# A graph attention kernel: node inputs and target logits in one DRAM row, one broadcast load for the turned rows, loads in another order

## The chip, the core and the metric

The kernel runs on one core of a Trainium2 chip. The metric is the device time of one execution in microseconds (us). PE is TensorE, DVE VectorE, ACT ScalarE, POOL GpSimd and SP SyncE, which here only issues DMAs. Before the change three runs took 2981.59, 2987.33 and 2987.8 us, a median of 2987.33.

## The reference, cut to what matters

There are 12,500 nodes with 128 inputs each and 200,000 edges, sorted by their destination `dst`; N and E are these two numbers.

```python
h = maximum(layernorm(x), 0)
hn = (h @ W_node.T).reshape(N, 4, 32)              # 4 heads of 32
e = (edge_attr @ W_edge.T).reshape(E, 4, 32)
att = sum(concat([hn[src], hn[dst], e], -1) * a, -1)
att = where(att > 0, att, 0.2 * att)
m = maximum(segment_max(att, dst), 0)
ex = exp(att - m[dst])
denom = segment_sum(ex, dst) + (E - deg)[:, None] * exp(-m)
w = ex / denom[dst]
out = x + segment_sum(w[:, :, None] * hn[src], dst).reshape(N, 128)
```

Here `deg` is the number of edges that end in a node.

## The kernel before, in words

A logit is a sum of a source part, a target part and an edge part, so the first two are made once for each node. The node stage (`load_nodes`, `node_statistics`, `node_scaled`, `turn_nodes`, `node_values`) goes through 11 sets of up to 9 tiles of 128 nodes: it loads x (L356), normalizes it, multiplies by the weights on PE, and stores two tables to DRAM. `table` has 137 floats a node: the values of the four heads, ones, and the source logits. `tgt` has the target logit as three bf16 pieces of four heads, 24 bytes a node (L394 to L399).

Edges are cut into 392 groups of 511, each with a leading slot that carries the group before over, 512 slots in all. Four groups make a quad (98 quads). Four quads make a round with one softmax (fewer at both ends; 28 rounds). The destinations of a group lie in a window of 96 nodes, whose first node is a number in SBUF (`base`); SP reads it into a register (L465) to address its loads and stores.

POOL gathers the rows of the source nodes: 16 indirect DMAs a quad (L135) into one of 8 buffers. The first four quads are gathered from x instead, before the node tables exist, and converted on the core (`converted`). A buffer comes free when its quad's last sum has been made (L638).

`fetch(q)` issues the loads of a quad on SP, two quads ahead of the logits: the edges' inputs `ea` (L472, 512 KB), the destinations broadcast to 96 partitions `db` (L474, 768 KB), and for each of the four groups the window's target logits `sw` (L480, 96 rows of 24 bytes) and the window's rows of x, `xw` (L481, 96 rows of 512 bytes). `db` has two buffers: its load waits until the comparison of the quad two back has read it (DVE L505). `xw` has eight.

`logits(q, i)` makes one group's logits: DVE compares destinations with the window (L505, into `at`), PE multiplies `at` by `sw` (L510) and the edges by their weights (L513). `add_sources` adds the gathered source part. `softmax(s)` handles a round: logits are turned on PE so that edges lie along the free axis, running maxima are scanned on DVE with the help of `dr`, the destinations in rows, which `fetch_rows` loads with four DMAs of the same rows, one a head (L489); exponentials are made on ACT and turned back (L601, L609).

`sums(q)` then takes a quad's four groups: DVE scales the gathered rows (L661) and makes the one-hot matrix (L664), and PE sums rows by destination (L669, three of four matmuls). The fourth (L638, in `complete_group`) needs the previous group's last row, which ACT takes out of PSUM (L639) and DVE scales (L633). `divide` makes the quad's output, adds x from `xw` (L692), and stores it with four DMAs (L694), each of which waits for the one before, since windows overlap.

The order of the work is written out by hand: generators are stepped in turn by `together`, and each engine runs its instructions in the order in which they were recorded. In the steady part one step pairs `sums(p)` with `all_logits(p + 5)`, whose first act is `fetch(p + 7)`; the closing quad of a round has `softmax` in the same step. On SP a step is therefore the loads of `fetch(p + 7)`, then the four stores of quad p - 1.

Of the kernel before, what the change touches and what calls it, by code (L numbers as in the profile page):

```python
# [8 lines left out]
F32 = mybir.dt.float32  # L9
BF16 = mybir.dt.bfloat16  # L10
# [5 lines left out]
P = 128  # L16
# [15 lines left out]
QG = 4  # L32
SBG = 16
PIECES = 3
NODE_T = 9
RAW = 4
SETS = max(NODE_T, QG * J)
# [8 lines left out]
def kernel(  # L46
# [42 lines left out]
    dram = ctx.enter_context(tc.tile_pool(name="dram", bufs=1, space=bass.MemoryType.DRAM))  # L89

    table = dram.tile([NP, ROW], F32, name="table")
    tgt = dram.tile([NP, PIECES, H], BF16, name="tgt")

    ident = consts.tile([P, P], F32, name="ident")
    make_identity(nc, ident)
# [50 lines left out]
    with tc.manual_schedule():  # L146
# [32 lines left out]
        def statistics(pool, rows, T):  # L179

            stats = pool.tile([P, SETS, nc.vector.BN_STATS_DIM], F32, name="stats")
            mv = pool.tile([P, SETS, nc.vector.BN_AGGR_DIM], F32, name="mv")
            for t in range(T):
                nc.vector.bn_stats(stats[:, t, :], rows[:, t, :])
                nc.vector.bn_aggr(mv[:, t, :], stats[:, t, :])  # L185
                if t % 3 == 2 or t == T - 1:
                    yield
            rstd = pool.tile([P, SETS], F32, name="rstd")
            nc.scalar.activation(rstd[:, :T], mv[:, :T, 1], AF.Sqrt, bias=eps)
            nc.vector.reciprocal(rstd[:, :T], rstd[:, :T])  # L190
# [69 lines left out]
        with tc.tile_pool(name="node", bufs=2) as node, tc.tile_pool(  # L260
# [91 lines left out]
            def load_nodes(b):  # L352
                if b < len(sets):
                    t0, T = sets[b]
                    XT[b] = node.tile([P, NODE_T, D], F32, name="xt", bufs=4)
                    nc.sync.dma_start(XT[b][:, :T, :], by_tile(x, t0, T))  # L356

            def node_statistics(b):
                if b < len(sets):
                    MV[b] = yield from statistics(node, XT[b], sets[b][1])  # L360

            def node_scaled(b):
                if b < len(sets):
                    HN[b] = node.tile([P, NODE_T, D], F32, name="hn", bufs=2)
                    yield from scaled(HN[b], XT.pop(b), sets[b][1], *MV.pop(b))

            waiting = []

# [9 lines left out]
            def node_values():  # L378
                b, t1, m, hT, row = waiting.pop(0)
                row_ps = node_ps.tile([P, 512], F32, name="row_ps")  # L380
                row_ps = row_ps[:, 0:3 * 160].rearrange("p (t r) -> p t r", r=160)
                for t in range(m):
                    nc.tensor.matmul(row_ps[:, t, :TCOL], hT[:, t, :], wcat, start=True, stop=True)  # L383
                nc.scalar.copy(row[:, t1:t1 + m, :], row_ps[:, :m, :TCOL])
                t0, T = sets[b]
                if t1 + m < T:
                    return
                one = row[:, :T, 0:H * HW].rearrange("p t (h w) -> p t h w", w=HW)[:, :, :, HD]
                nc.vector.memset(one, 1.0)
                nc.vector.memset(row[:, :T, R_CNT:R_CNT + 1], 1.0)  # L390
                nc.sync.dma_start(by_tile(table, t0, T), row[:, :T, 0:ROW])
                tp = node.tile([P, NODE_T, PIECES, H], BF16, name="tp")
                tg = row[:, :T, ROW:TCOL]
                for k in range(PIECES):  # L394
                    nc.vector.tensor_copy(tp[:, :T, k, :], tg)
                    if k < PIECES - 1:
                        nc.vector.tensor_tensor(tg, tg, tp[:, :T, k, :], op=OP.subtract)
                nc.scalar.dma_start(by_tile(tgt.rearrange("n k h -> n (k h)"), t0, T),
                                    tp[:, :T].rearrange("p t k h -> p t (k h)"))  # L399

            for b in range(3):
                load_nodes(b)
# [42 lines left out]
    with tc.tile_pool(name="load", bufs=3) as load, tc.tile_pool(name="work", bufs=2) as work, \  # L445
            tc.tile_pool(name="turned", bufs=1) as turned, \
            tc.tile_pool(name="ps", bufs=1, space=bass.MemoryType.PSUM) as ps:
        EA, DB, SW, XW, LG, AT, U, DR = {}, {}, {}, {}, {}, {}, {}, {}


        const_ps = ps.tile([P, WIN + G + QG * H], F32, name="const_ps")
# [17 lines left out]
        def fetch(q):  # L469
            g0, m = quads[q]  # L470
            ea = EA[q] = load.tile([P, QG, 2, P], F32, name="ea")
            nc.sync.dma_start(ea[:, :m], edge_t[:, g0:g0 + m])  # L472
            db = DB[q] = load.tile([WIN, QG, GE], I32, name="db", bufs=2)
            nc.sync.dma_start(db[:, :m, :], dst.rearrange("(g e) -> g e", e=GE)[g0:g0 + m]  # L474
                              .unsqueeze(0).to_broadcast([WIN, m, GE]))
            sw = SW[q] = load.tile([WIN, QG, PIECES * H], BF16, name="sw")
            xw = XW[q] = load.tile([WIN, QG, D], F32, name="xw", bufs=8)
            for i in range(m):
                w = window(g0 + i)
                nc.sync.dma_start(sw[:, i, :], tgt[bass.ds(w, WIN)].rearrange("n k h -> n (k h)"))  # L480
                nc.sync.dma_start(xw[:, i, :], x[bass.ds(w, WIN), :])  # L481
            if q not in GA:
                gather(q, table, ROW)

        def fetch_rows(s):
            g0, m = groups(s)
            dr = DR[s] = turned.tile([SBG * H, NE + 2], I32, name="dr", bufs=2)
            for h in range(H):
                nc.sync.dma_start(dr[h * m:(h + 1) * m, :], dst_rows[g0:g0 + m, :])  # L489

        def open_logits(q):
            if q == supers[of_quad[q]][0]:
# [6 lines left out]
        def logits(q, i):  # L499

            g0, m = quads[q]
            if i >= m:
                return
            ea, db, sw, at, lg = EA[q], DB[q], SW[q], AT[q], LG[q]
            nc.vector.tensor_tensor(  # L505
                at[:, i, :], node_ps[0:WIN, g0 + i:g0 + i + 1].to_broadcast([WIN, GE]), db[:, i, :],
                op=OP.is_equal)
            for w in range(2):
                for j in (2 * w, 2 * w + 1):
                    nc.tensor.matmul(lg[:, i, j].rearrange("p k h -> p (k h)"),  # L510
                                     at[:, i, j * P:(j + 1) * P], sw[:, i, :],
                                     start=i + j == 0, stop=False, skip_group_check=True)
                nc.tensor.matmul(lg[:, i, 2 * w:2 * w + 2, 0, :], ea[:, i, w, :], wblk,  # L513
                                 start=False, stop=True, skip_group_check=True)

        def add_sources(q):

            s = of_quad[q]
            g0, m = quads[q]
            s0, sm = groups(s)  # L520
            if s not in U:
                U[s] = turned.tile([P, J, SBG * H], F32, name="U", bufs=2)
            u = U[s][:, :, 0:sm * H].rearrange("p j (h g) -> p g j h", h=H)[:, g0 - s0:g0 - s0 + m]
            st = work.tile([P, QG, J, H], F32, name="st")
            nc.vector.tensor_reduce(st[:, :m], LG[q][:, :m].rearrange("p g j k h -> p g j h k"),
                                    AX.X, OP.add)
            nc.vector.tensor_tensor(u, st[:, :m], GA[q][:, :m, :, R_SRC:R_SRC + H], op=OP.add)
            for kept in (EA, DB, SW, AT, LG):
                del kept[q]

        XS = {}
# [142 lines left out]
        def divide(q, pt):  # L674
# [14 lines left out]
            nc.vector.tensor_tensor(  # L689
                res[:, :m, :].rearrange("p g (h d) -> p g h d", d=HD), val[:, :, :, 0:HD],  # L690
                share_ps[:, :m, :].unsqueeze(3).to_broadcast([WIN, m, H, HD]), op=OP.mult)
            nc.vector.tensor_tensor(res[:, :m, :], res[:, :m, :], xw[:, :m, :], op=OP.add)  # L692
            for i in range(m):
                nc.sync.dma_start(out[bass.ds(window(g0 + i), WIN), :], res[:, i, :])  # L694

# [50 lines left out]

    redo = nc.values_load(flag[0:1, 0:1], min_val=0, max_val=1)
    with tc.If(redo > 0):
        tile_any_order(tc, x, src, dst, edge_t, table, tgt, wblk, ident, part, out, by_tile, E)


@with_exitstack
def tile_any_order(ctx, tc, x, src, dst, edge_t, table, tgt, wblk, ident, part, out, by_tile, E):

# [31 lines left out]
    with tc.For_i(0, EP // (2 * P), 1) as pair:  # L786
# [4 lines left out]
        for c in range(2):  # L791
# [5 lines left out]
            nc.vector.tensor_scalar(dfl, di, float(NP - 1), None, op0=OP.min)  # L797
            nc.vector.tensor_copy(di, dfl)
            ga = pool.tile([P, ROW], F32, name="any_ga")
            tg = pool.tile([P, PIECES * H], BF16, name="any_tg")  # L800
            st = pool.tile([P, ROW], F32, name="any_st")
            for o, i, ix in ((ga, table, si), (tg, tgt.rearrange("n k h -> n (k h)"), di),
                             (st, states[0:NP], di)):
                nc.gpsimd.indirect_dma_start(
                    out=o, out_offset=None, in_=i,
                    in_offset=bass.IndirectOffsetOnAxis(ap=ix[:, 0:1], axis=0))
# [4 lines left out]
            att = pool.tile([P, H], F32, name="any_att")  # L811
            nc.vector.tensor_tensor(att, lg[:, c, :], ga[:, R_SRC:R_SRC + H], op=OP.add)
            for k in range(PIECES):
                nc.vector.tensor_tensor(att, att, tg[:, k * H:(k + 1) * H], op=OP.add)
            nc.vector.scalar_tensor_tensor(att, att, SLOPE, att, op0=OP.mult, op1=OP.max)


# [125 lines left out]
```

## Time and profile before

| what | us |
|---|---|
| median of three runs | 2987.33 |
| the profiled execution | 3018.5 |
| its span | 3016.7 |
| first gathers, from x (64) | 2.9 to 82.8 |
| first gathers from `table` (64) | 185.3 to 265.5 |
| the other 1438 gathers, in batches of 16 | 339.9 to 2873.0 |

In a line of groups or of the timeline, `out<-in` are the program's tile names, and brackets hold the engine's idle time before the instruction and what ended it. In a line of waits the numbers are the total in us, the times and the longest. A line of the busy times by stretch has the stretch, its length, then busy us and number of instructions of PE, PE's weight loads, DVE, ACT and POOL, the granted clock of PE, the busy share of the 16 DMA engines, and GB/s. "remote" stands for a wait whose end the trace can't put down to an instruction or a DMA. Rows named SPq are DMA issues on SP; a register move or a register load is not shown in the timeline, but is in the trace. A batch's distance is from one batch's first gather to the next one's.

### The profile page before, as it was taken

The page shows a single profiled execution, that of the slowest core. Times are in us where ns is not written, and L with a number is a line of the kernel's source. Part 1 is how long each engine was busy: PE and PEld are TensorE (multiplying, and loading weights), DVE is VectorE, ACT ScalarE, POOL GpSimd, SP SyncE. Part 2 cuts the span into 40 slices and gives each one's busy share as a digit, 9 for nine tenths or more (in the row PEclk, how much of TensorE's full clock was granted, in tenths as well). Part 3 has the DMA queues.
Part 4 walks back from the last instruction along what each step waited for, and adds up shares of the span by engine and source line. Part 5 has one row for each costly group of instructions (what it writes and reads, how often), then busy time and mean ns, then how long its engine had stood idle before and what let it go on. Part 6 is the DMA issues. An engine that isn't in the chain of part 4 may idle for free.

```text
span 3016.7 us, 29229 instructions
## 1 busy us (share of the span) xinstructions
PE 1411.3 (47%) x7275; PEld 1268.1 (42%) x7275; DVE 1381.7 (46%) x3438; ACT 424.0 (14%) x1764; POOL 1498.2 (50%) x1574
## 2 busy tenths in 40 slices
PE   1541645444444544544544444454454444444464
PEld 1431544344444444434434444444444444444354
DVE  1741454444544544544444443454454444444466
ACT  1431311111110111111111111011111111111111
POOL 7043245556556555555555555555555555555500
PEclk9755655555555555555555555555555555555555
DMA  3632454344344344444444434434444344444320
GB/s 113 115 75 70 110 126 107 94 108 110 96 102 109 97 100 110 101 104 102 102 103 103 107 98 104 108 96 105 106 105 106 97 110 103 98 108 101 83 57 15
DMA packets 228078, 299.11 MB, mean 99 GB/s; under 512 B 89081, under 2 KB 177273, under 8 KB 218498
## 3 DMA queue, kind: packets, MB, share of 16 engines
q1 hardware_dynamic: 174512, 184.67, 23.9%
q0 software_dynamic: 50112, 109.65, 16.2%
q10 hardware_dynamic: 3282, 2.89, 0.4%
q8 instruction: 61, 1.00, 0.1%
q14 instruction: 111, 0.91, 0.1%
HBM read 270.49 MB, written 26.52 MB: 98 GB/s over the span
## 4 chain that ended last, share of the span: by engine, by line
another core or an unknown queue 30%; PE 29%; DVE 12%; issue 9%; ACT 5%; ACTq 0%; DMA 0%; SPq 0%; DVEq 0%
PE acc L669 15%; PE lg L513 6%; PE acc L638 5%; DVE res L689 2%; DVE at L505 2%; DVE res L692 2%; ACT pt L639 2%; DVE run L578 1%; PE lg L510 1%; PE t_ps L547 1%; ACT ga L657 1%; DVE run L556 1%; ACT ga L637 1%; DVE top L584 1%
## 5 line engine op out<-in xcount | busy, mean ns | idle before, releaser
L135 POOL DMA_INDIRECT ga<-table,srci x1502 | 1436.6, 956 | 1353.6 <-PE acc L638 817.6
L669 PE MATMUL acc<-ga,hot 128*97 128x137 f32 x2352 | 652.8, 450 | 753.5 <-ACT ga L657 648.6
L669 PEld LDWEIGHTS acc<-ga,hot 128*97 128x97 f32 x2352 | 523.3, 281 | 778.3 <-ACT ga L657 656.8
L633 DVE TENSOR_TENSOR ga<-pt,facs 1x132 f32<-1x132 f32 x391 | 112.3, 287 | 988.5 <-ACT pt L639 797.0
L639 ACT COPY pt<-acc 97x137 f32<-97x137 f32 x392 | 107.5, 274 | 2144.4 <-remote 1087.1
L513 PE MATMUL lg<-wblk,ea 128*128 128x8 f32 x1568 | 408.7, 359 | 0.0
L510 PEld LDWEIGHTS <-at 96*128 96x128 bf16 x1568 | 214.8, 166 | 423.2 <-DVE at L505 246.8
L513 PEld LDWEIGHTS lg<-wblk,ea 128*128 128x128 f32 x1568 | 381.7, 309 | 0.0
L510 PE MATMUL lg<-sw,at 96*128 96x12 bf16 x1568 | 169.1, 181 | 353.8 <-DVE at L505 220.9
L638 PE MATMUL acc<-ga,hot 128*97 128x137 f32 x784 | 263.3, 439 | 151.6 <-issue 88.4
L661 DVE TENSOR_TENSOR ga<-ga,ex_ps 128x528 f32<-128x528 f32 x392 | 270.4, 690 | 59.2 <-ACT xs L611 58.9
L505 DVE TENSOR_TENSOR at<-const_ps,db 96x512 bf16<-96x512 f32 x392 | 266.5, 682 | 26.5 <-DMA xw<-in_x_dram 10.5
L638 PEld LDWEIGHTS acc<-ga,hot 128*97 128x97 f32 x784 | 194.2, 281 | 168.9 <-issue 98.3
L664 DVE TENSOR_TENSOR hot<-const_ps,slot 128x384 f32<-128x384 f32 x392 | 214.0, 546 | 0.0
L683 DVE TENSOR_TENSOR den<-den,others 96x16 f32<-96x16 f32 x98 | 16.7, 171 | 265.6 <-ACT den L682 168.1
L383 PE MATMUL row_ps<-wcat,hT 128*128 128x141 f32 x198 | 52.0, 429 | 84.1 <-issue 30.6
L383 PEld LDWEIGHTS row_ps<-wcat,hT 128*128 128x128 f32 x198 | 43.6, 302 | 92.6 <-issue 54.5
L637 ACT COPY ga<-pt 1x1 f32<-1x1 f32 x391 | 73.4, 188 | 9.8
L601 PE MATMUL ex_ps<-ident,ex 64*128 64x64 f32 (+2 forms) x112 | 18.4, 312 | 116.1 <-ACT ex L590 116.1
L135 POOL DMA_INDIRECT ga<-in_x_dram,srci x64 | 60.7, 948 | 20.6 <-issue 19.2
L185 DVE BATCH_NORM_AGGREGATE mv<-stats 128x2 f32<-128x6 f32 x163 | 29.7, 182 | 87.6 <-remote 64.2
L692 DVE TENSOR_TENSOR res<-res,xw 96x512 f32<-96x512 f32 x98 | 67.3, 687 | 3.4
(128 smaller groups left out, 1087.1 us busy)
## 6 DMA issues: line engine op xcount, KB each, us to landing
db<-in_dst_dram SPq DMA_DIRECT2D x98, 768.0 KB
ea<-in_edge_t_dram SPq DMA_DIRECT2D x98, 512.0 KB
ga<-table,srci POOLq DMA_INDIRECT x1502
xw<-in_x_dram SPq DMA_DIRECT2D x392, 48.0 KB
out_dram<-res SPq DMA_DIRECT2D x392, 48.0 KB
table<-row SPq DMA_DIRECT2D x11, 616.5 KB
xt<-in_x_dram SPq DMA_DIRECT2D x11, 576.0 KB
sw<-tgt SPq DMA_DIRECT2D x392, 2.2 KB
```

The source lines that it names most:

```text
L135: nc.gpsimd.indirect_dma_start(out=ga[:, i, j, 0:width], out_offset=None, in_=rows, in_offset=bass.IndirectOffsetOnAxis(ap=srci[:, g0 + i, ...
L505: nc.vector.tensor_tensor(at[:, i, :], node_ps[0:WIN, g0 + i:g0 + i + 1].to_broadcast([WIN, GE]), db[:, i, :], op=OP.is_equal)
L510: nc.tensor.matmul(lg[:, i, j].rearrange("p k h -> p (k h)"), at[:, i, j * P:(j + 1) * P], sw[:, i, :], start=i + j == 0, stop=False, skip ...
L513: nc.tensor.matmul(lg[:, i, 2 * w:2 * w + 2, 0, :], ea[:, i, w, :], wblk, start=False, stop=True, skip_group_check=True)
L633: nc.vector.tensor_tensor(ga[0:1, i, 0, 0:H * HW].rearrange("p (h w) -> p h w", w=HW), before[WIN:WIN + 1, 0:H * HW].rearrange("p (h w) -> ...
L637: nc.scalar.copy(ga[0:1, i, 0, R_CNT:R_CNT + 1], before[WIN:WIN + 1, R_CNT:R_CNT + 1])
L638: nc.tensor.matmul(acc, hot[:, i, 0, :], ga[:, i, 0, :], start=False, stop=True)
L639: nc.scalar.copy(pt[:, i, :], acc)
L661: nc.vector.tensor_tensor(val, val, heads(ex)[:, :, :, g - s0].unsqueeze(3).to_broadcast([P, J, H, HW]), op=OP.mult)
L664: nc.vector.tensor_tensor(hot[:, i, :, 0:WIN], lane_ps.unsqueeze(1).to_broadcast([P, J, WIN]), slot[:, g, :].unsqueeze(2).to_broadcast([P, ...
L669: nc.tensor.matmul(acc, hot[:, i, j, :], ga[:, i, j, :], start=j == 1, stop=False)
L692: nc.vector.tensor_tensor(res[:, :m, :], res[:, :m, :], xw[:, :m, :], op=OP.add)
```

## The change

Every DRAM row of the new tensor `side` has a node's 128 inputs and its three target pieces: 134 floats, 536 bytes. In the node stage x is loaded into the first 128 columns of a wider tile with five buffers instead of four, the pieces are written behind them, and the whole tile is stored by ACT's queue where `tgt` was stored. In `fetch`, one load of 96 rows of 536 bytes takes the place of the loads of `sw` and `xw`; these four loads now stand ahead of `db`. L510 takes its right side from the end of the `xw` row. `fetch_rows` loads `dr` by one DMA whose source is broadcast over the heads. In the changed file the line numbers are one higher as far as `fetch` (L472 is L473) and one lower behind it (L505 is L504, L638 is L637); in `fetch` the joined load is L476, `db` is L478 and `dr` L486.

```diff
+SIDE = D + PIECES * H // 2
...
-    tgt = dram.tile([NP, PIECES, H], BF16, name="tgt")
+    side = dram.tile([NP, SIDE], F32, name="side")
...
-                    XT[b] = node.tile([P, NODE_T, D], F32, name="xt", bufs=4)
-                    nc.sync.dma_start(XT[b][:, :T, :], by_tile(x, t0, T))
+                    XT[b] = node.tile([P, NODE_T, SIDE], F32, name="xt", bufs=5)
+                    nc.sync.dma_start(XT[b][:, :T, 0:D], by_tile(x, t0, T))
...
-                tp = node.tile([P, NODE_T, PIECES, H], BF16, name="tp")
+                xt = XT.pop(b)
+                tp = xt[:, :T, D:SIDE].bitcast(BF16).rearrange("p t (k h) -> p t k h", h=H)
...
-                nc.scalar.dma_start(by_tile(tgt.rearrange("n k h -> n (k h)"), t0, T),
-                                    tp[:, :T].rearrange("p t k h -> p t (k h)"))
+                nc.scalar.dma_start(by_tile(side, t0, T), xt[:, :T, :])
...
             nc.sync.dma_start(ea[:, :m], edge_t[:, g0:g0 + m])
+            xw = XW[q] = load.tile([WIN, QG, SIDE], F32, name="xw", bufs=8)
+            for i in range(m):
+                nc.sync.dma_start(xw[:, i, :], side[bass.ds(window(g0 + i), WIN), :])
             db = DB[q] = load.tile([WIN, QG, GE], I32, name="db", bufs=2)
             nc.sync.dma_start(db[:, :m, :], dst.rearrange("(g e) -> g e", e=GE)[g0:g0 + m]
                               .unsqueeze(0).to_broadcast([WIN, m, GE]))
-            sw = SW[q] = load.tile([WIN, QG, PIECES * H], BF16, name="sw")
-            xw = XW[q] = load.tile([WIN, QG, D], F32, name="xw", bufs=8)
-            for i in range(m):
-                w = window(g0 + i)
-                nc.sync.dma_start(sw[:, i, :], tgt[bass.ds(w, WIN)].rearrange("n k h -> n (k h)"))
-                nc.sync.dma_start(xw[:, i, :], x[bass.ds(w, WIN), :])
...
-            for h in range(H):
-                nc.sync.dma_start(dr[h * m:(h + 1) * m, :], dst_rows[g0:g0 + m, :])
+            nc.sync.dma_start(dr[0:H * m, :],
+                              dst_rows[g0:g0 + m, :].unsqueeze(0).to_broadcast([H, m, NE + 2]))
...
+            sw = XW[q][:, i, D:SIDE].bitcast(BF16)
```

More of the change, by code (lines that the diff above doesn't have):

```diff
@@ L354, in load_nodes @@
                     t0, T = sets[b]
-                    XT[b] = node.tile([P, NODE_T, D], F32, name="xt", bufs=4)
-                    nc.sync.dma_start(XT[b][:, :T, :], by_tile(x, t0, T))
+                    XT[b] = node.tile([P, NODE_T, SIDE], F32, name="xt", bufs=5)
+                    nc.sync.dma_start(XT[b][:, :T, 0:D], by_tile(x, t0, T))
             def node_statistics(b):
                 if b < len(sets):
-                    MV[b] = yield from statistics(node, XT[b], sets[b][1])
+                    MV[b] = yield from statistics(node, XT[b][:, :, 0:D], sets[b][1])
             def node_scaled(b):
@@ L364, in node_scaled @@
                     HN[b] = node.tile([P, NODE_T, D], F32, name="hn", bufs=2)
-                    yield from scaled(HN[b], XT.pop(b), sets[b][1], *MV.pop(b))
+                    yield from scaled(HN[b], XT[b][:, :, 0:D], sets[b][1], *MV.pop(b))
             waiting = []
@@ L391, in node_values @@
                 nc.sync.dma_start(by_tile(table, t0, T), row[:, :T, 0:ROW])
-                tp = node.tile([P, NODE_T, PIECES, H], BF16, name="tp")
+                xt = XT.pop(b)
+                tp = xt[:, :T, D:SIDE].bitcast(BF16).rearrange("p t (k h) -> p t k h", h=H)
                 tg = row[:, :T, ROW:TCOL]
                 for k in range(PIECES):
-                    nc.vector.tensor_copy(tp[:, :T, k, :], tg)
+                    nc.vector.tensor_copy(tp[:, :, k, :], tg)
                     if k < PIECES - 1:
-                        nc.vector.tensor_tensor(tg, tg, tp[:, :T, k, :], op=OP.subtract)
-                nc.scalar.dma_start(by_tile(tgt.rearrange("n k h -> n (k h)"), t0, T),
-                                    tp[:, :T].rearrange("p t k h -> p t (k h)"))
+                        nc.vector.tensor_tensor(tg, tg, tp[:, :, k, :], op=OP.subtract)
+                nc.scalar.dma_start(by_tile(side, t0, T), xt[:, :T, :])
             for b in range(3):
@@ L447 @@
             tc.tile_pool(name="ps", bufs=1, space=bass.MemoryType.PSUM) as ps:
-        EA, DB, SW, XW, LG, AT, U, DR = {}, {}, {}, {}, {}, {}, {}, {}
+        EA, DB, XW, LG, AT, U, DR = {}, {}, {}, {}, {}, {}, {}
         const_ps = ps.tile([P, WIN + G + QG * H], F32, name="const_ps")
@@ L503, in logits @@
                 return
-            ea, db, sw, at, lg = EA[q], DB[q], SW[q], AT[q], LG[q]
+            ea, db, at, lg = EA[q], DB[q], AT[q], LG[q]
+            sw = XW[q][:, i, D:SIDE].bitcast(BF16)
             nc.vector.tensor_tensor(
@@ L510, in logits @@
                     nc.tensor.matmul(lg[:, i, j].rearrange("p k h -> p (k h)"),
-                                     at[:, i, j * P:(j + 1) * P], sw[:, i, :],
+                                     at[:, i, j * P:(j + 1) * P], sw,
                                      start=i + j == 0, stop=False, skip_group_check=True)
@@ L527, in add_sources @@
             nc.vector.tensor_tensor(u, st[:, :m], GA[q][:, :m, :, R_SRC:R_SRC + H], op=OP.add)
-            for kept in (EA, DB, SW, AT, LG):
+            for kept in (EA, DB, AT, LG):
                 del kept[q]
@@ L691, in divide @@
                 share_ps[:, :m, :].unsqueeze(3).to_broadcast([WIN, m, H, HD]), op=OP.mult)
-            nc.vector.tensor_tensor(res[:, :m, :], res[:, :m, :], xw[:, :m, :], op=OP.add)
+            nc.vector.tensor_tensor(res[:, :m, :], res[:, :m, :], xw[:, :m, 0:D], op=OP.add)
             for i in range(m):
@@ L748, with tile_any_order @@
     with tc.If(redo > 0):
-        tile_any_order(tc, x, src, dst, edge_t, table, tgt, wblk, ident, part, out, by_tile, E)
+        tile_any_order(tc, x, src, dst, edge_t, table, side, wblk, ident, part, out, by_tile, E)
 @with_exitstack
-def tile_any_order(ctx, tc, x, src, dst, edge_t, table, tgt, wblk, ident, part, out, by_tile, E):
+def tile_any_order(ctx, tc, x, src, dst, edge_t, table, side, wblk, ident, part, out, by_tile, E):
     nc = tc.nc
@@ L799, in tile_any_order @@
             ga = pool.tile([P, ROW], F32, name="any_ga")
-            tg = pool.tile([P, PIECES * H], BF16, name="any_tg")
+            tg = pool.tile([P, SIDE], F32, name="any_tg")
             st = pool.tile([P, ROW], F32, name="any_st")
-            for o, i, ix in ((ga, table, si), (tg, tgt.rearrange("n k h -> n (k h)"), di),
+            for o, i, ix in ((ga, table, si), (tg, side, di),
                              (st, states[0:NP], di)):
@@ L813, in tile_any_order @@
             for k in range(PIECES):
-                nc.vector.tensor_tensor(att, att, tg[:, k * H:(k + 1) * H], op=OP.add)
+                nc.vector.tensor_tensor(att, att, tg[:, D:SIDE].bitcast(BF16)[:, k * H:(k + 1) * H],
+                                        op=OP.add)
             nc.vector.scalar_tensor_tensor(att, att, SLOPE, att, op0=OP.mult, op1=OP.max)
```

## The prediction

> **What bounds the kernel now.** I read the page's busy times first, then the waits, then the busy times of one round of four quads, then the instructions of one quad in order of time.
>
> ```profile
> span 3016.7 us, 29229 instructions
> PE 1411.3 (47%) x7275; PEld 1268.1 (42%) x7275; DVE 1381.7 (46%) x3438; ACT 424.0 (14%) x1764; POOL 1498.2 (50%) x1574
> ```
>
> No engine is busy for more than half of the span, so a cycle of waits sets the pace. The waits (engine, line, what ended the wait: us in total, times, longest) name two of its links:
>
> ```profile
> ACT pt L639 <- remote: 1087.1, 89, 18.6
> POOL ga L135 <- PE acc L638: 817.6, 89, 74.5
> ```
>
> Both occur 89 times, about once a quad (98 quads): POOL waits for TensorE's last sum of a quad (L638), which frees a gather buffer, and ACT waits some 12 us for something that the trace doesn't name. One round, quad by quad:
>
> ```profile
> 1466.30:1492.40 26.10, 12.33 (x65) 11.24 (x66) 10.66 (x24) 2.73 (x15) 15.35 (x17) 0.50 0.44 104
> 1492.40:1518.50 26.10, 12.49 (x65) 11.18 (x66) 10.68 (x24) 2.69 (x15) 15.33 (x16) 0.50 0.46 109
> 1518.50:1544.60 26.10, 12.35 (x66) 11.26 (x66) 10.95 (x26) 2.78 (x15) 15.38 (x16) 0.50 0.48 109
> 1544.60:1578.10 33.50, 15.81 (x83) 13.67 (x84) 18.27 (x43) 4.68 (x20) 15.14 (x16) 0.55 0.37 93
> ```
>
> Three quads of 26.1 us and a closing one, with the softmax, of 33.5: 111.7 us a round. Each stretch starts with a batch of 16 gathers. The second in order of time:
>
> ```profile
> 1505.30 0.74 PE L638 MATMUL acc<-ga,hot 128*97 128x137 f32 x2 [1.23 <-ACT pt L639]
> 1505.94 0.34 SPq L474 DMA_DIRECT2D db<-in_dst_dram  x1
> 1507.15 0.33 SPq L480 DMA_DIRECT2D sw<-tgt  x1
> 1509.58 0.69 SPq L481 DMA_DIRECT2D xw<-in_x_dram  x1
> 1511.36 0.95 POOL L135 DMA_INDIRECT ga<-table,srci  x1 [0.30 <-issue]
> 1513.10 0.72 SPq L480 DMA_DIRECT2D sw<-tgt  x1
> 1515.42 0.32 SPq L480 DMA_DIRECT2D sw<-tgt  x1
> 1515.45 0.27 ACT L639 COPY pt<-acc 97x137 f32<-97x137 f32 x1 [10.35 <-remote]
> 1517.61 0.66 PE L638 MATMUL acc<-ga,hot 128*97 128x137 f32 x2
> 1518.54 0.95 POOL L135 DMA_INDIRECT ga<-table,srci  x1 [6.24 <-PE acc L638]
> ```
>
> The third group's sum ends at 1506.04 by the trace, yet its reader on ACT starts at 1515.45. The trace's times of the semaphore that TensorE's matmuls raise say the same: nothing between 1504.58 and 1515.26, then five raises 0.04 us apart. SP crawls meanwhile: even its register moves, which touch no memory, take 0.70 us each instead of 0.03. Both end together, about 3 us after the batch's last gather (1511.36 + 0.95). Then the fourth group passes at once (1515.45 to 1518.27), POOL starts the next batch, and it repeats. So a normal quad is 16 gathers of 0.95 us with pauses of 0.30 (20.0 us), some 2.7 us until the signals come through, and 3.4 us for the last group: 26.1 us.
>
> What starts and ends the crawl matters most, as the removed loads lie in it (L480, L481). Two observations speak for the gathers. First, by these times the crawl's end follows the batch's start by 22.6 to 22.8 us in nearly every normal quad, however far SP has come. Second, between 185 and 266 us the 64 first gathers run, SP issues nothing at all, and the same crawl is there:
>
> ```profile
> ACT ga L252 <- remote: 70.3, 4, 31.6
> ```
>
> (the waits between 185 and 285 us). So I take it to belong to the gathers, not to SP's loads.
>
> **The change part by part.** Of SP's work per quad, four loads go (sw, 96 rows of 24 bytes), each with two register instructions: 12 of 51 instructions. A sw load and the register work to the next load take 0.50 us outside the crawl (1541.39 to 1541.89) and 2 to 2.4 us in it. The Trainium skill's DMA: Bandwidth & Descriptors (Rules for kernel authors) says that transfers under 64 KB are mostly overhead and should be joined; sw is 2.2 KB. Taken as time on the path, 392 loads of 0.50 us would be 196 us. The trace puts them on an engine on which nothing waits in the steady part: the only waits that name sw are two of 18.2 us in all, at 293 and 425 us. By the row they are worth 0 there, and I take the row.
>
> The joined row is 536 bytes. Its nearest packet is the table's 548-byte one, 29 to 32 ns in the stage at 116 us, against 27 + 9 ns for the 512- and 24-byte packets that it replaces: nothing lost.
>
> The order becomes ea, four xw, db, then the stores. By the built program the first xw load now waits for DVE L692 of an older quad, because it comes ahead of the db wait that used to cover it. Queued behind it on SP are three more xw loads, db and four stores. L692 ends at 1523.9 in this round (ea went out at 1523.26), the four loads need 4 x 0.83 us (1.32 us for a pair now, less 0.50), so SP is ready for db at 1527.2; db waits for DVE L505 until 1530.66 anyway. Cost 0, covered by 3.4 us; without the cover, db and the stores slip by as much, and db's reader is more than a quad away. The stores move from 1544 into the crawl; nobody waits on them within a quad (res has two buffers).
>
> The dr loads go from four to one in each of 28 rounds: 3 x 0.4 us of SP, unwaited. The same section says that a leading broadcast dimension of 4 confines a DMA to 4 engines. By that rule each engine moves 16 rows instead of 4; at the 84 to 101 ns of dr's 2052-byte packets 1.5 instead of 0.4 us. L542 reads dr a whole round later: 0 by the trace.
>
> The stage before 185 us gains work. The x load writes rows of 512 bytes in place of 4608 (per engine 72 x 0.027 = 1.9 us against 8 x 0.2 = 1.6), and a 603 KB store replaces one of 27 KB, 11 times. The nearest row, the table's stores, takes 2 to 4 us of the queues for the same bytes. The DMA engines are busy 0.58 of 82 to 185 us, so +1.5 to +3 us in each 9 us still fits, and loads run three sets ahead. Bounds 0 and +8 us (the last stores reaching POOL's start); I take +1, as nothing in that stage waits for a load.
>
> Where SP is waited for is the start. DVE's first comparisons of quads 0, 1 and 2 wait for db (start, us, what, idle before):
>
> ```profile
> 292.99 2.48 DVE L505 TENSOR_TENSOR at<-const_ps,db 96x512 bf16<-96x512 f32 x4 [10.49 <-DMA xw<-in_x_dram]
> 300.69 2.48 DVE L505 TENSOR_TENSOR at<-const_ps,db 96x512 bf16<-96x512 f32 x4 [2.23 <-DMA db<-in_dst_dram]
> 309.99 0.69 DVE L505 TENSOR_TENSOR at<-const_ps,db 96x512 bf16<-96x512 f32 x1 [3.85 <-DMA db<-in_dst_dram]
> ```
>
> Each comes about 7 us after its issue (285.75, 293.63, 302.93), paced by SP's 7.9 us a quad. After the change a quad takes SP about 0.4 + 3.3 + 0.4 + 0.4 = 4.5 us. The first db goes out 3.3 us later, the second at the old time, the third some 4 us earlier (then gated by DVE); from quad 3 on compute paces. Gain about 4 us there, and some 4 more at 409 to 426 us, where the chain runs through SP's loads and stores and a 6.87 us landing of sw: -8 (bounds 0 and -20).
>
> Normal quads, 64 or so: 0 if the crawl's end is fixed, at best -0.5 each, if the 12 instructions would otherwise share the stretch after it (71 instructions in 1541.4 to 1544.6, 0.045 us each); I take -0.1, or -6. Closing quads, 22: SP has 28 fewer instructions after the crawl (db to stores at 1567 on), at most -1.2 each; the softmax on DVE sets this stretch, so -0.3, or -7.
>
> Sum: +1 - 8 - 6 - 7 = -20 us. On the profiled execution (3018.5 us, 1.8 of it outside the span) that is 2998.5. It lies 31.2 us above the median of the runs (2987.33), so by the same difference 2967.
>
> **The rivals.** *SP's instructions help to hold the crawl.* For: db, sw and xw lie inside it, and a stall begins within 0.2 us of db in most quads. Against: the end's fixed distance. If the crawl ends 0.5 to 1.2 us earlier in 85 quads, -42 to -100, with the start 2885 to 2935. If it vanished, normal quads would fall to the gathers' 20.1 us and the time towards 2550; the stretch at 185 us speaks against that.
>
> *Slower: the xw loads reach the crawl earlier.* They now stand 5.4 to 8.7 us into a batch, and the second group's signal begins to lag from about 8 us on (its L638 ended at 1501.6, its reader started at 1504.61, 12.2 us in). If SP's 16 instructions at 0.70 us take turns with TensorE's there, that signal comes up to 11 us later. It decides once it is later than about 19 us into the batch, as then two groups instead of one remain after the crawl: +2.9 us a quad (1518.31 to 1521.22). In a third of the quads, 30 x 2.9 = 87 less the gain of 8: about 3066; in a few, 3005. The margin is 7 us.
>
> *The change does nothing that counts.* The start's gain is eaten by the node stage: 2985.
>
> **How the numbers follow.** My forecast, the cycle stays and the start and closing quads gain: 0.50, at 2950 to 2983. The crawl thins: 0.20. It breaks: 0.05. Slower: 0.16, from 2995 up. Nothing: 0.09. About 0.2% (6 us) is what a measurement tells from no change. Faster 0.43 + 0.20 + 0.05 = 0.68; same 0.06 + 0.07 = 0.13; slower 0.16 + 0.03 = 0.19. For 8 in 10 the range goes from 2900, most of the thinning case, to 3010, its mild slower cases; left out are the break and the strong slowing.
>
> **What would show it.** Right: normal quads still 26.1 us from batch to batch with a wait of about 6.2 us on POOL, ACT L639's unnamed wait still over 1000 us, db issued at the old place, and quad 2's first comparison near 306 us. Wrong: batches less than 25.5 or more than 28 us apart, closing quads off 33.5 by more than 1, or POOL's first table gather later than 190 us.

## The result and the profile after

| | median us | range | ratio to before (95% interval) |
|---|---|---|---|
| before, 20 runs | 2987.47 | 2981.59 to 2997.09 | |
| changed, 20 runs | 2991.72 | 2984.6 to 2996.56 | 1.0013 (1.0005 to 1.0021) |

The change doesn't make the kernel faster: it costs some 4 us, at the edge of what can be measured. Two later comparisons, on two chips, gave 1.0010 (1.0004 to 1.0017) and 1.0013 (1.0005 to 1.0021).

The page of the changed kernel has fewer instructions and a shorter span than the page of before:

```profile
span 2992.2 us, 27935 instructions
```

The 24.5 us between the two spans (3016.7 and 2992.2) look like the forecast of -20, but they can't be compared. The profiled execution of before (3018.5) lies outside the range of its 20 runs; every later profiled execution is one of its kernel's timed runs. The kernel before, profiled once more (e1 below), spans 3003.9 us and took 3005.72, in a group of runs with a median of 3008.31. And the median of before differs from one group of runs to the next: 2987, 3008, 3013, 3018. So in what follows times and profiles are set against each other within a group as far as there are such.

The waits of the changed kernel are the ones that the prediction named, with about the same totals:

```profile
ACT pt L638 <- remote: 1108.8, 101, 18.7
POOL ga L136 <- PE acc L637: 788.7, 89, 74.3
```

One round, by the busy times of its four stretches:

```profile
1449.00:1474.80 25.80, 12.57 (x65) 11.26 (x66) 10.73 (x25) 2.76 (x15) 15.37 (x17) 0.50 0.41 97
1474.80:1500.70 25.90, 12.57 (x65) 11.27 (x66) 10.68 (x24) 2.77 (x15) 15.38 (x17) 0.50 0.46 109
1500.70:1526.40 25.70, 12.51 (x65) 11.20 (x66) 10.97 (x26) 2.71 (x15) 15.35 (x16) 0.50 0.45 113
1526.40:1559.60 33.20, 15.50 (x83) 13.36 (x84) 18.30 (x43) 4.71 (x20) 15.13 (x17) 0.55 0.37 89
```

The cycle stands: three quads and a closing one, each 0.2 to 0.4 us shorter than in the first profile of before. One and the same kernel shows as much from group to group. Means over the 64 normal and 21 closing quads from the fourth batch of 16 on (without the last, shorter one) are 26.07 and 33.58 us in the first profile of before and 25.97 and 33.49 in its second; the changed kernel has 25.82 and 33.41 here, but 26.04 and 33.98 in e5. All means of quads below are taken like this.

At the start the loads moved as forecast. DVE's first comparisons of quads 0, 1 and 2 (start, us, what, idle before):

```profile
294.37 2.48 DVE L504 TENSOR_TENSOR at<-const_ps,db 96x512 bf16<-96x512 f32 x4 [12.18 <-DMA db<-in_dst_dram]
300.90 2.48 DVE L504 TENSOR_TENSOR at<-const_ps,db 96x512 bf16<-96x512 f32 x4 [1.05 <-DMA db<-in_dst_dram]
307.74 0.69 DVE L504 TENSOR_TENSOR at<-const_ps,db 96x512 bf16<-96x512 f32 x1 [1.39 <-DMA db<-in_dst_dram]
```

They were at 292.99, 300.69 and 309.99: the first later, the second the same, the third earlier.

### The profile page after: what moved, and what is told of

Same layout as the page of the kernel before. It is cut to its first block, busy times and chain, and to the rows that moved or that the text cites. A ratio compares the mean times of both kernels' runs of the same rounds, so it can differ in the third digit from the quotient of the medians.

```text
span 2992.2 us, 27935 instructions
## 1 busy us (share of the span) xinstructions
PE 1428.5 (48%) x7275; PEld 1265.1 (42%) x7275; DVE 1382.5 (46%) x3438; ACT 423.7 (14%) x1764; POOL 1498.1 (50%) x1574
## 4 chain that ended last, share of the span: by engine, by line
PE 33%; another core or an unknown queue 29%; DVE 13%; issue 9%; ACT 5%; ACTq 0%; SPq 0%; DMA 0%; DVEq 0%
PE acc L668 18%; PE lg L512 7%; PE acc L637 3%; DVE at L504 2%; DVE res L691 2%; DVE res L688 2%; ACT pt L638 1%; DVE run L577 1%; PE lg L509 1%; DVE run L555 1%; PE t_ps L546 1%; ACT ga L656 1%; ACT ga L636 1%; DVE top L583 1%
## 5 line engine op out<-in xcount | busy, mean ns | idle before, releaser
L632 DVE TENSOR_TENSOR ga<-pt,facs 1x132 f32<-1x132 f32 x391 | 112.4, 288 | 974.3 <-ACT pt L638 695.9
L638 ACT COPY pt<-acc 97x137 f32<-97x137 f32 x392 | 107.4, 274 | 2127.3 <-remote 1108.8
L637 PE MATMUL acc<-ga,hot 128*97 128x137 f32 x784 | 265.3, 441 | 238.9 <-issue 158.9
L509 PE MATMUL lg<-xw,at 96*128 96x12 bf16 x1568 | 168.5, 180 | 340.1 <-DVE at L504 314.4
L637 PEld LDWEIGHTS acc<-ga,hot 128*97 128x97 f32 x784 | 190.0, 278 | 269.7 <-issue 178.7
L504 DVE TENSOR_TENSOR at<-const_ps,db 96x512 bf16<-96x512 f32 x392 | 266.8, 683 | 20.4 <-DMA db<-in_dst_dram 14.6
L136 POOL DMA_INDIRECT ga<-in_x_dram,srci x64 | 60.7, 948 | 20.7 <-issue 19.2
L688 DVE TENSOR_TENSOR res<-pt,const_ps 96x512 f32<-96x512 f32 x98 | 66.9, 683 | 3.7 <-DVE const_ps L686 0.3
```

Source lines behind the costliest of these rows:

```text
L136: nc.gpsimd.indirect_dma_start(out=ga[:, i, j, 0:width], out_offset=None, in_=rows, in_offset=bass.IndirectOffsetOnAxis(ap=srci[:, g0 + i, ...
L504: nc.vector.tensor_tensor(at[:, i, :], node_ps[0:WIN, g0 + i:g0 + i + 1].to_broadcast([WIN, GE]), db[:, i, :], op=OP.is_equal)
L632: nc.vector.tensor_tensor(ga[0:1, i, 0, 0:H * HW].rearrange("p (h w) -> p h w", w=HW), before[WIN:WIN + 1, 0:H * HW].rearrange("p (h w) -> ...
L637: nc.tensor.matmul(acc, hot[:, i, 0, :], ga[:, i, 0, :], start=False, stop=True)
L638: nc.scalar.copy(pt[:, i, :], acc)
L688: nc.vector.tensor_tensor(res[:, :m, :].rearrange("p g (h d) -> p g h d", d=HD), val[:, :, :, 0:HD], share_ps[:, :m, :].unsqueeze(3).to_br ...
```

## The experiments

"The hold" in the expectations is what the prediction calls the crawl. Each ratio is to the kernel before, timed on the same chip in the same group of runs; the groups' medians of before stand in the headings.

### The parts alone (before: 3008.11)

**e1**, the kernel before itself. 

> The kernel before, unchanged, profiled once more and timed against itself. Theory A (the 24.5 us between the two profiled executions are what the change does, and the timed runs lose them elsewhere): the profile again spans about 3016 us, with normal quads 26.1 us apart and closing quads 33.5. Theory B (the first profiled execution of before was slow by itself, by some 0.3 us a quad that no timed run pays): a span of 2980 to 2995, normal quads 25.7 to 25.9. The timed ratio is 1.000, and its interval is the width that the other comparisons have: some 0.0015 either way.

Measured: 1.0002 (0.9992 to 1.0011), span 3003.9, normal quads 25.97. The span and the quads lie between the two theories, on a chip whose runs of this kernel are 21 us longer than those of the first group. What speaks for theory B is the place among its own runs: this profiled execution is 2.6 us below its median, the first one was 31 above.

**e2**, before with the one load of `dr`:

```diff
-            for h in range(H):
-                nc.sync.dma_start(dr[h * m:(h + 1) * m, :], dst_rows[g0:g0 + m, :])
+            nc.sync.dma_start(dr[0:H * m, :],
+                              dst_rows[g0:g0 + m, :].unsqueeze(0).to_broadcast([H, m, NE + 2]))
```

> Before, with the one broadcast load of dr alone. It takes 84 loads from SP, which nothing waits for. Both theories: within 2 us of before. If the broadcast on few queues disturbed the softmax rounds, 28 rounds by 0.1 to 0.4 us: up to +11.

Measured: 1.0020 (1.0011 to 1.0028), some 6 us: the expectation's last case by its size. In the profile 5 of 21 closing quads take more than 33.75 us (1 in e1), and their mean is 33.67 instead of 33.49, which makes 4 us; most of the rest by which its span is longer lies ahead of the fourth batch (461.0 us instead of 455.2). What the load of `dr` does to these quads isn't shown.

**e3**, before with the four `sw` and four `xw` loads moved ahead of `db`. 

> Before, with the eight loads sw and xw of a quad ahead of db in place of behind it. By the prediction's sum the start loses: a quad still takes SP 7.9 us and the first db goes out about 7 us later: +3 to +7. If the loads ahead of db also reach the crawl (the rival that ends slower): +30 to +90, with normal quads of up to 29 us in the profile. If the order does nothing: 0 +- 2.

Measured: 1.0037 (1.0024 to 1.0050), some 11 us, between the expectations. Normal quads are 26.05 us (25.97 in e1), but closing quads 34.47 instead of 33.49, and all 21 are above 33.75: a place that no theory had named. The profiled execution is the slowest of its eight runs, 17 us above their median, so the runs pay less than it shows.

**e4**, the joined row alone: the change with `db` ahead of `xw` and with the loop of e2. 

> The joined row alone: one load of 536 bytes in place of two, db first as before, dr by four loads as before. By the prediction's sum: +1 for the node stage, -8 to -12 at the start, -6 and -7 in the quads, so about -20. If the node stage pays for the wider store (0 to +8) and nothing else answers: +1 to +8. If theory B holds (the quads are paced by the gathers alone): -10 to +5, with the profile's quads at the same 25.8 as those of before.

Measured: 0.9981 (0.9973 to 0.9988), with the quads of e1 (25.97 and 33.45): within theory B's range, and not the gain of 20 that the prediction's sum gives.

### The parts together (before: 3012.80)

**e5**, the changed kernel. 

> The changed kernel itself, on the same chip as its parts. What the parts gave so far: the joined row -5.7 (ratio 0.9981), dr alone +6.0 (1.0020), the order alone, with eight loads, +11 (1.0037). Theory C (the parts add up: the joined row gains a little, dr and the order give it back): a ratio of 1.0005 to 1.0030. Theory D (each chip has its own times, and the change is worth what the two first profiles say): 0.9920.

Measured: 1.0010 (1.0004 to 1.0017): theory C.

**e6**, the change with `dr` by four loads. 

> The change without its dr part: joined row, its four loads ahead of db, dr by four loads. Theory C with dr to blame: a ratio of about 0.998, as the joined row alone, and 6 us below the changed kernel. With the order to blame as well (four loads put eight register instructions and four issues into the crawl of the closing quads): 1.000 to 1.002, with some closing quads of 34.5 us in the profile in place of 33.5.

Measured: 1.0010 (1.0003 to 1.0017), with 12 of 21 closing quads above 33.75 us: `dr` isn't to blame.

**e7**, the change with `db` ahead of `xw`. 

> The change without its order: joined row, db first, dr by one broadcast load. If dr costs what it cost alone: 0.9981 + 0.0020, about 1.000. If dr's price was one of the eight loads behind it: 0.998.

Measured: 0.9977 (0.9967 to 0.9986). So joined row and broadcast gain 7 us together, and the order of `xw` and `db` gives 11 back (3016.61 in e5 less 3005.74). The price of `dr` in e2 doesn't come back here. In the profiles a closing quad takes 33.98 us on average in e5 and 33.50 in e7; above 33.75 are 12 of 21 in e5 and none in e7. That is 21 x 0.49 = 10 us. The normal quads add 64 x 0.04 = 3 (26.04 against 26.00).

### Where the order costs (before: 3017.99)

**e13**, the changed kernel, with `db` first again in the closing quads only:

```diff
-            xw = XW[q] = load.tile([WIN, QG, SIDE], F32, name="xw", bufs=8)
-            for i in range(m):
-                nc.sync.dma_start(xw[:, i, :], side[bass.ds(window(g0 + i), WIN), :])
+            closing = q >= 2 and q - 2 == supers[of_quad[q - 2]][0]
+            if not closing:
+                rows()
             db = DB[q] = load.tile([WIN, QG, GE], I32, name="db", bufs=2)
...
+            if closing:
+                rows()
```

(`rows` holds the three lines taken out.) 

> The changed kernel with db first in the closing quads alone, once more. Under the hold (before at about 3000 us): theory E, the order costs in the closing quads: a ratio of 0.996 to 0.998 and closing quads of 33.5 us; theory F, it costs elsewhere: 1.000 to 1.001. Without the hold (before at about 2166): 1.000, as before.

**e14**, the changed kernel beside it. 

> The changed kernel beside it. Under the hold: 1.001 again. Without the hold nothing displaces TensorE's signals: by theory E the order then costs nothing, and the joined row gains little where SP has time: 0.998 to 1.001, and no more than 0.1% from the kernel that keeps db first in the closing quads.

Measured: e13 0.9955 (0.9941 to 0.9968), a little below theory E's range, and e14 1.0013 (1.0005 to 1.0021). In the steady part the order has its price in the closing quads: above 33.75 us are 1 of 21 in e13 (mean 33.53) and 12 of 21 in e14 (33.96), which makes 9 us. Normal quads are the same (26.07 and 26.08). The two profiled executions are 15.8 us apart; 5.6 of that lie ahead of the fourth batch (445.2 and 450.8 us), where e13's edit changes the quads of the first rounds too, and the granted clock was higher (0.61 against 0.56 from 285 to 340 us). The medians are 20.7 apart; where the runs that weren't profiled have the rest isn't shown.

A closing quad of e14 in order of time; the batch of gathers starts at 1426.31:

```profile
1429.74 0.27 ACT L638 COPY pt<-acc 97x137 f32<-97x137 f32 x1 [1.16 <-PE acc L637]
...
1432.44 8.97 SPq L476 DMA_DIRECT2D xw<-side  x4
...
1437.46 0.66 PE L637 MATMUL acc<-ga,hot 128*97 128x137 f32 x2
...
1449.24 0.27 ACT L638 COPY pt<-acc 97x137 f32<-97x137 f32 x1 [18.77 <-remote]
1449.54 0.29 DVE L632 TENSOR_TENSOR ga<-pt,facs 1x132 f32<-1x132 f32 x1 [10.28 <-ACT pt L638]
1449.86 0.69 DVE L504 TENSOR_TENSOR at<-const_ps,db 96x512 bf16<-96x512 f32 x1
1450.47 0.14 DVE L576 COPY col<-ex_ps 64x1 f32<-64x1 f32 x1
1450.58 0.32 SPq L478 DMA_DIRECT2D db<-in_dst_dram  x1
```

The sum of the second group is done at 1438.12 (1437.46 + 0.66), and ACT gets it at 1449.24, 22.9 us into the batch. Two instructions of DVE wait for it, L632 and, in line behind it, L504; the softmax's next step L576 stands behind both. In e13 the batch starts at 1530.04 and SP sends nothing between `ea` and `db`:

```profile
1533.47 0.28 ACT L646 COPY pt<-acc 97x137 f32<-97x137 f32 x1 [1.16 <-PE acc L645]
...
1541.18 0.66 PE L645 MATMUL acc<-ga,hot 128*97 128x137 f32 x2
...
1545.03 0.27 ACT L646 COPY pt<-acc 97x137 f32<-97x137 f32 x1 [10.83 <-issue]
1545.34 0.29 DVE L640 TENSOR_TENSOR ga<-pt,facs 1x132 f32<-1x132 f32 x1 [2.60 <-issue]
1545.65 0.69 DVE L512 TENSOR_TENSOR at<-const_ps,db 96x512 bf16<-96x512 f32 x1
1546.37 0.32 SPq L484 DMA_DIRECT2D db<-in_dst_dram  x1
1547.79 6.10 SPq L478 DMA_DIRECT2D xw<-side  x4
...
1552.84 0.15 DVE L584 COPY col<-ex_ps 64x1 f32<-64x1 f32 x1 [6.50 <-remote]
```

The second group's sum passes at 15.0 us, its two DVE instructions are done while the crawl lasts, and the softmax's step starts at 22.8 us, as soon as the crawl ends, in place of 24.2. In all closing quads of e14 the line is sharp: copy at 21.3 us or earlier, 33.4 to 33.6 us from batch to batch; at 21.9 to 22.1, 33.8 to 33.9; at 22.7 to 22.9, 34.5 to 34.8.

**e15**, e7 with eight loads of 32 bytes (`extra`, nobody reads them) ahead of `db` in the closing quads. 

> Joined row, broadcast dr, db first, and eight loads of 32 bytes ahead of db in the closing quads alone, once more. Under the hold: theory E (any of SP's instructions displaces the signal): closing quads of 33.9 to 34.7 and 1.000 to 1.003; otherwise 0.998. Without the hold: 1.001, as before.

Measured: 1.0000 (0.9992 to 1.0009), 0.0023 above e7, which ran on another chip; 8 of 21 closing quads above 33.75, mean 33.94. One of them, whose batch starts at 1540.82:

```profile
1543.77 5.41 SPq L477 DMA_DIRECT2D extra<-in_x_dram  x8
...
1563.64 0.27 ACT L642 COPY pt<-acc 97x137 f32<-97x137 f32 x1 [18.66 <-remote]
```

So it is not the `xw` loads as such: other loads of SP ahead of `db` do the same. The last of these is out 8.4 us into the batch and the copy starts at 22.8, so how they delay the signal is not shown.

### The same edits without the crawl (before: 2166.37, and 2168.10 in the last group)

**e9** and **e12** are the kernels of e13 and e15, run earlier. 

> The changed kernel, except that in the closing quad of a round (the step with the softmax) db goes ahead of the four xw loads again. In the profiles so far closing quads of 33.9 to 34.7 us come with the changed order (12 of 21, a mean of 33.9 to 34.0) and hardly ever without it (33.5). Theory E (the order costs its 10 us in the closing quads, where SP's instructions for xw go through the hold in place of TensorE's signal): closing quads back at 33.5, and a ratio of 0.996 to 0.998, as without the new order. Theory F (the order costs in the normal quads, or through the stores that now stand in the hold): 1.000 to 1.001, as the changed kernel.

> The joined row and the broadcast dr with db first (0.9977), and in the closing quads alone eight loads of 32 bytes ahead of db, which nobody reads: 21 times eight issues on SP. Theory E (any instruction of SP that goes through the hold there can displace TensorE's signal): closing quads of 33.9 to 34.7 again, and a ratio of 1.000 to 1.003. If it is the xw loads themselves that cost (their wait, or their rows): 0.998 to 0.999, closing quads at 33.5.

In this group the kernel before took 2166 us, and 2168 in the last one. The waits of e9 show why:

```profile
ACT pt L646 <- PE acc L645: 1373.6, 391, 12.4
PEld L517 <- DVE at L512: 557.8, 153, 5.7
PE lg L517 <- DVE at L512: 502.6, 152, 5.4
POOL ga L136 <- issue: 460.8, 1511, 0.6
```

These are its largest four: none is on "remote", and POOL waits for no sum. Between 460 and 2000 us SP's register moves take 0.03 us (0.04 at most), where in e13, the same kernel, 73 of 439 take over 0.3. The crawl is absent, and the gathers alone pace the quads, 16 in 20.3 us. Measured: e9 1.0006 (0.9993 to 1.0018), e12 1.0012 (1.0001 to 1.0023). They say nothing on theories E and F, hence e13 to e15.

### The cycle itself (before: 3012.80, 3017.99, 2166.37, 2168.10)

**e8**, e4 with a gather buffer for each group:

```diff
-        ga = GA[q] = gath.tile([P, QG, J, ROW], F32, name="ga")
+        GA[q] = []
         for i in range(m):
+            ga = gath.tile([P, J, ROW], F32, name="ga")
+            GA[q].append(ga)
```

(and 32 buffers; what reads the rows goes by group.) 

> The joined row alone (db first, dr by four loads), with a gather buffer for each group in place of one for each quad: POOL then waits for the sum of one group of a quad eight back, and gathers by four. Theory of the cycle (a batch of 16 gathers holds TensorE's signals back from about 8 us in until 2.7 us after its last gather): bursts of four gathers, 5 us, end before the hold begins, and a quad falls from 26 us towards the 20 us of its gathers, so that the time is 2400 to 2700. If the hold comes with any stretch of gathers, POOL runs on and the signals trickle through: between 2900 and 3200, with the wait in front of ACT's copy of the sum as long as before.

Measured: 0.9207 (0.9191 to 0.9222), 2770.94 us.

```profile
ACT pt L645 <- PE acc L644: 702.8, 192, 12.8
ACT pt L645 <- remote: 667.2, 87, 10.7
```

The unnamed wait falls from 1136 us (e1) to 667, and from 460 us on 16 gathers take 25.2 us on average, rounds included, in place of 27.7. Bursts are now of 4, 8 or 12 gathers, and with the longer ones the crawl still comes: a middle case between the two theories.

The bursts show what the crawl's end goes by. Here is one of 12, by its first gather and ACT's copy:

```profile
1414.51 0.95 POOL L138 DMA_INDIRECT ga<-table,srci  x1 [2.11 <-remote]
...
1431.83 0.27 ACT L645 COPY pt<-acc 97x137 f32<-97x137 f32 x1 [8.21 <-remote]
```

From 460 us on ACT's copy has 85 waits on "remote": 39 in bursts of 8, 44 in bursts of 12 and 2 in bursts of 4. By their medians they end 11.5 us behind the first gather of 8 and 17.3 behind that of 12; in e1, with batches of 16, it is 22.9. That is 1.43 to 1.45 us for each gather, where POOL issues one each 1.25. The end of the crawl moves with the number of gathers, as the prediction's reading has it; what takes the 1.43 us isn't shown.

**e16** and, without the crawl, **e10**: e8 with a one-element memset on POOL behind each gather. 

> A buffer per group, and a one-element memset on POOL behind each gather, once more. Under the hold: theory G (unseen work of the gathers falls behind, and spacing lets it catch up): 2350 to 2600 us, ratio 0.78 to 0.86; theory H (any long stretch of gathers holds): 2750 to 3000, 0.91 to 1.00. Without the hold: 0.995, as before.

> A buffer per group (2771 us), with a one-element memset on POOL behind every gather. The hold lasted to 22.7 us after a batch's start, which is 16 times 1.42, where POOL issues a gather each 1.25 us. Theory G (work of the gathers that the profile doesn't show falls behind POOL by 0.17 us each, and the hold lasts while it is behind): if the memset spaces gathers by 0.15 us or more, or waits for that work, the hold goes, ACT's unnamed waits (667 us) fall to under 200, and the time to 2350 to 2600. Theory H (the hold comes 8 us into any stretch of gathers without a long gap): the time rises with POOL's added work, 1500 x 0.1 to 0.2 us, to 2800 to 3000.

Measured: e16 0.9229 (0.9215 to 0.9243), e10 0.9955 (0.9935 to 0.9976). The memset (0.09 us) fell into the pause that was there already, so gathers still came every 1.25 us: the spacing that theory G asks for was not put to the test.

**e11**, e8 with a memset of 128 x 512 behind each fourth gather. 

> A buffer per group, with one memset of 128 x 512 floats on POOL behind every fourth gather, so that bursts of 5 us have a gap of some 0.5 to 1 us between them. Theory G: 2400 to 2650. Theory H, if such a gap is too short (2.1 to 2.8 us is what ends the hold now): 2771 plus up to 90, since 98 x 4 memsets add to POOL's work.

Measured without the crawl: 1.0481 (1.0463 to 1.0499), which is 105 us. Each of the 392 memsets takes 0.54 us on the engine that paces, and a part of it falls into the pause that was there: from gather to gather it is 1.65 us across a memset, in place of 1.25. It says nothing on theories G and H.

**e17**, e8 with all that had gained. 

> What the runs point to, in one kernel: the joined row, dr by one load, the new order except in closing quads (0.9955 by itself), and a gather buffer for each group (0.9207 with the joined row, which has 0.9981). Under the hold, if the two gains add: 0.916 to 0.921. If the new order's loads stand in the hold's way once bursts are short: 0.921 to 0.93. Without the hold: 0.99 to 1.00.

**e18**, before without every second quad's gathers. 

> The kernel before with half of its gathers left out: from the sixth quad on, each second quad takes the rows of the quad ahead of it and gathers nothing, so its sums are of other nodes; every other instruction stays. If the hold belongs to the gathers, a quad without gathers has no unnamed wait in front of ACT's copy of the sum: the total of those waits falls from about 1100 to 400 to 700 us, such a quad takes 14 to 20 us, and the time is 2450 to 2800. If the hold comes with SP's loads, which all stay, the waits stay at 1000 to 1200 us and the time at 2900 to 3010. Without the hold (before at about 2166): 1700 to 2000, by the gathers that are gone.

Both fell where there is no crawl: e17 0.9922 (0.9903 to 0.9940), e18 0.9075 (0.9054 to 0.9095). What e17 gives under the crawl, and what e18 was to show, a quad without gathers under the crawl, stay open.

## Why the prediction was wrong

**The bound** was right for the runs that have the crawl: the cycle of batch, crawl and last group sets the pace (three times 26.1 and 33.5 make 111.8 us a round, where the text has 111.7), removing a quarter of SP's instructions left it where it was, and loosening its link to POOL (e8) gave 8%.

**The node stage**, +1: POOL's first gather from `table` came at 186.4 us in e5 and 184.1 in e1, within the bounds.

**The start**, -8: right in e6 and e13, whose fourth batch stands at 447.3 and 445.2 us against 455.2 in e1. In e5 and e14 it was 454.1 and 450.8. The clock that TensorE was granted from 285 to 340 us differs between these profiles, from 0.53 (e5) to 0.61 (e13). At an equal 0.59, e6 is 7.9 us ahead of e1, on another chip; that the clock makes the rest of the differences isn't shown. So the term is known no better than -1 to -10.

**The joined loads**, 0 in the steady part by the trace's row. The rule of the Trainium skill's DMA: Bandwidth & Descriptors (Rules for kernel authors), that transfers under 64 KB are mostly overhead and should be joined, made 196 us in the prediction, had each load's 0.50 us been on the path. e4 gained 5.7 us and e7, with `dr`, 6.9, the start included. The row was the right one to take.

**The `dr` load**, 0: alone it cost 6 us (e2), beside the joined row nothing (e7). On how many DMA engines it ran, no trace here shows.

**Normal quads**, -6: they gained nothing. The crawl's end is fixed, as the text had it, and taking instructions off SP did not shorten what follows (25.97 us in e1 and in e4). The order costs them 0.04 us (e5 against e7).

**Closing quads**, -7: this is the term that failed. It counted what SP does after the crawl and took DVE's softmax for the bound; it did not ask what the moved loads do inside the crawl in that quad. They cost 10 us (e5 against e7) and 9 (e14 against e13). For the 20 runs above the price is less certain: their profiled execution has only two such quads (34.47 and 34.71 us among 33.2 to 33.5), not 12, which makes some 3 us.

**The slower rival** had the effect: loads ahead of `db` make the second group's signal later. That SP's instructions take turns with it, as it says, is not shown (e15). In normal quads the second group's signal moved from 10.4 us into the batch (e1) to 13.4 (e5), as the rival said, and that is nearly free, as the bound was 19. But "the margin is 7 us" was read in a normal quad only. In the closing quads of e1 the signal already came at 15.6 to 22.1 us, and there it decides from about 22 us on, at up to 1.3 us a quad. The first profile had it in the very round that was shown, whose closing batch starts at 1544.60:

```profile
1565.98 0.27 ACT L639 COPY pt<-acc 97x137 f32<-97x137 f32 x1 [17.21 <-remote]
```

That is 21.4 us into the batch: a margin of half a microsecond. One other closing quad of that profile was already beyond it, at 22.8, and took 34.61 us. With the terms as e5 and e7 have them, the sum is +1 - 8 + 3 + 10 = +6, against +4 in the 20 runs; with closing quads as in the first profile of the changed kernel it would be about -1. So no trace here shows all of the +4.

## What to carry to other kernels

Check the margin of a moved step in the tightest stretch of a round, not in the most frequent one: the same four loads cost next to nothing in each of 64 quads and half a microsecond on average in each of 21. Where an order may have two effects, split it by place: with `db` first again in the closing quads, the changed kernel went from 0.13% above before to 0.45% below it. Before a span is compared with another, see that each profiled execution lies within the times of its own kernel's runs, and take both in one group of runs.

## What the runs showed of the hardware

The crawl is not always there. On one chip the kernel before took 3008 us in one group of runs and 2166 in a later one; in two of six groups it was absent, on two chips. With it, 16 gathers of one and the same kernel take 27.9 us from 460 us on (e13), without it 20.3 (e9), at the same 1.25 us from gather to gather within a batch. The throughput of the DMA engines isn't what is missing: they move 141 GB/s in e9 and 102 in e13. What turns it on isn't shown by any trace here; it is worth 840 us, two hundred times the change that was studied.
